# Three moves in the order of a two-layer graph kernel: one gate's sums, one product step's pieces, the late gates' last operations

## The chip, the cores and the metric

The kernel runs on one core of one Trainium2 chip. Its time is the device time of one execution in microseconds (us). Three runs of the kernel before gave 2016.03, 2013.95 and 2015.03 us; the median, 2015.03 us, is the time that the change is compared with. TensorE (PE), VectorE (DVE), ScalarE (ACT), GpSimd (POOL) and SyncE (SP, which only issues DMAs here) each run their own list of instructions in order; what one engine needs from another it waits for by semaphores.

## The reference

64 graphs of 256 nodes with 256 features go through two layers, each with a residual and a layernorm:

```python
x = _layernorm(x + _L0_gnn_ref(x, adj, ...))
# layer 0: deg = adj.sum(-1); norm_adj = deg**-0.5 * adj * deg**-0.5 (rows, columns)
#          ((norm_adj + alpha * I) @ x) @ W.T + b
x = _layernorm(x + _L1_gnn_ref(x, mask, ...))
# layer 1: h = relu(bn1(conv1(xT)));  h = bn2(conv2(h))       17 taps over the nodes
#          x_conv = relu(h + xT).T
#          s = x @ w_se.T + b_se;  A = exp(-|s_n - s_m|**2)
#          msg = relu(x @ w_msg.T + b_msg);  x_nmp = A @ msg
#          GRU: gi = [x_conv, x_nmp] @ w_ih.T,  gh = x @ w_hh.T
#          r, z = sigmoid(gi + gh);  n = tanh(gi_n + r * gh_n)
#          (1 - z) * n + z * x
```

## The kernel before, in words

**Work and groups.** The 64 graphs are taken in four groups of 16 (`Q = 16`), because the 17-tap convolution is computed by a discrete Fourier transform of length 48 over tiles of 32 nodes, with one product for each frequency over the tiles of all 16 graphs of a group. For each graph, `layer0` (L418 on) and `layer1` (L513 on) are generators that are advanced piece by piece; `graphs` interleaves them, so that layer 0 of graph g + 2 runs beside layer 1 of graph g.

- In layer 0, ACT sums the degrees, POOL takes the power deg**-0.5 (`dis`, L438), PE transposes the adjacency matrix (L449), ACT copies it to `adjT` (L450), DVE adds the diagonal (L452), ACT scales x (L467), POOL adds the bias to x_t (L470), PE multiplies (p_hT L475, p_out L485), DVE adds the residual (L491) and `layernorm` follows: two bn_stats (L372), two bn_aggr (L373), `ln_rs` (DVE L374, then a power on POOL, L375), `ln_mr` (L379), and ACT's normalising (L392).
- In layer 1, PE does conv1 (L526), msg (L547) and the transform (p_dft L565); DVE makes the squares (L536 to L539, the last of them `scols`); PE transposes those (p_rows L578), ACT copies them out (L581), PE multiplies distances (p_dist L588), ACT takes exp into `aT` (L589), DVE multiplies aT by the adjacency matrix (L592), and PE sums the messages with it (p_nmp L601). The last DVE and ACT instructions of some of these, of the newest graph, are kept in dictionaries: SQUARED (L539), DIAGONAL (L452), WEIGHED (L592), CONV1, EXP and so on.

**The transform.** For each group q, 12 steps (`PAIRS`) multiply the frequencies (p_k L632). The inverse transform works in place on one tile, VM: `real_transform`, then from step 4 on `complex_begin(step)` (pieces at L686, L687, L691, L692), then `complex_end` (pieces at L718 to L728, L824 and others, and DMAs of its outputs to xc_d at L825). For the first group (q = 0), three pieces of the next group's graphs (`begin`) are run with each step, and the transform's pieces of that step are queued behind the newest graph's SQUARED, DIAGONAL and WEIGHED operations, by `issue_after`. When the steps are over, `paced` advances `complex_end` by a due amount whenever a marked operation of the other work is passed.

**The gate.** `gru(g)` (L966 on) multiplies a graph's inputs by the gate weights as seven half-size products of a Strassen scheme (p_g L982), whose sums of inputs are made ahead on POOL (`sums1` to `sums4`, `input_sums`, L941): gate g makes those of gate g + 1. DVE joins products (L1004, L1014, L1020, L1062), ACT takes two tanh (L1033, L1049), DVE mixes (L1039 to L1048). What remains is the last product and subtraction, `rest()` (L959, L960), and a layernorm of the output (`normed`). Up to the third group, `rest()` and the first part of that layernorm, down to the power on POOL, are run when the next gate begins; in the last group (`g >= B - Q`) they are run in `mixed` and `finished` of the gate itself.

The first gates of a group (`EARLY = (4, 4, 1, Q)`: four, four, one, all) run beside the group's own later graphs or at once; the others of the first three groups, the late gates (4 to 15, 20 to 31, 33 to 47), run beside the steps and graphs of the next group. The order in which each engine gets its instructions is then set by a scheduler from priorities, dependencies and the `issue_after` edges; what stands where in an engine's queue is its result.

Of the kernel before, what the change touches and what calls it, by code (L numbers as in the profile page):

```python
# [26 lines left out]
def kernel(  # L27
# [938 lines left out]
    def gru(g):  # L966

        following = g % Q + 1 < Q  # L970
        inputs, S = GATE.pop(g), SUMS.pop(g)
        G = gate.tile([P, NCH, 2, 4, HD], F32, name="G", bufs=1)
        if following:
            load_gate(g + 1)
        A11, A12, A21, A22 = halves(inputs)

        def product(a, b, p=None):
            first = p is None
            if first:
                p = accbank("p_g")  # L980
            for k in range(HALF):
                nc.tensor.matmul(  # L982
                    p[:, : 3 * HD] if k == 0 else p[:, HD:], a[:, k], wall[:, b, k].rearrange("p t d -> p (t d)"),
                    start=first and k == 0, stop=True, skip_group_check=not first or k > 0,
                )
            return p

        def quarter(c, h):
            return G[:, c, h].rearrange("p t d -> p (t d)")

        p1 = product(A11, B11)
        first = gate.tile([P, 4 * HD], F32, name="first", bufs=1)
        nc.scalar.copy(first, p1)
        p7 = product(S[3], T3)
        yield
        if following:
            sent(g + 1)
        if REST:
            rest()
            next(NORMS[-1])  # L1000
        with tc.issue_after(CONV1[max(CONV1)]) if in_blocks(g) and g < B - Q else ExitStack():
            p6 = product(S[2], T2)
        mark(nc.vector.tensor_add(quarter(0, 1), first, p6), 1)
        nc.vector.tensor_add(quarter(1, 1), quarter(0, 1), p7)  # L1004
        product(A12, B21, p1)
        own = nc.scalar.copy(quarter(0, 0), p1).ins  # L1006
        sooner = following and in_blocks(g + 1) and g < B - Q
        if sooner:
            transposed(g + 1)
        yield  # L1010
        if following and not sooner:
            transposed(g + 1)
        p5 = product(S[1], T1)
        joined = nc.vector.tensor_add(quarter(1, 1), quarter(1, 1), p5)  # L1014
        mark(joined, 1)
        with tc.issue_after(own), tc.issue_after(joined.ins):
            ended()
        load_x1(g)
        product(A22, T4, p7)
        mark(nc.vector.tensor_add(quarter(1, 0), quarter(0, 1), p7), 1)  # L1020
        if following:
            input_sums(g + 1, 3, 1, 2)
        yield
        product(S[4], B22, p5)
        if following:
            input_sums(g + 1, 4)
        if g % Q + 2 < Q:
            load_conv(g + 2)
        x1 = OWN.pop(g)

        def squashed(c, cols=slice(0, 2)):
            rz = G[:, c, cols, GR : GZ + 1, :].rearrange("p h t d -> p h (t d)")
            nc.scalar.activation(rz, rz, AF.Tanh, scale=0.5)  # L1033

        def mixed(part, cols=slice(0, 2)):
            both = G[:, part, cols].rearrange("p c h t d -> p (c h) t d")
            chunks = G[:, part].shape[1]
            r, z, n, i = (both[:, :, j, :] for j in (GR, GZ, GN, GI))
            nc.vector.scalar_tensor_tensor(n, r, 1.0, n, op0=ALU.add, op1=ALU.mult)  # L1039
            i4 = i.rearrange("p (c h) d -> p c h d", c=chunks)  # L1040
            bias = bn_t.rearrange("p (h d) -> p h d", h=2)[:, cols]
            nc.vector.tensor_tensor(
                i4, i4, bias.unsqueeze(1).to_broadcast([P, chunks, bias.shape[1], HD]), op=ALU.add
            )
            MIXED[0] = nc.vector.scalar_tensor_tensor(i, n, 0.5, i, op0=ALU.mult, op1=ALU.add).ins
            y = x1[:, part]
            yq = y.rearrange("p c (h d) -> p c h d", h=2)[:, :, cols].rearrange("p c h d -> p (c h) d")
            mark(nc.vector.scalar_tensor_tensor(yq, z, 3.0, yq, op0=ALU.add, op1=ALU.mult), 1)  # L1048
            nc.scalar.activation(i, i, AF.Tanh)  # L1049
            REST.append((z, i, yq))  # L1050
            if g >= B - Q:
                rest()
            return y

        def finished(part, y):
            NORMS.append(normed(g, part, y))
            if g >= B - Q:
                next(NORMS[-1])

        if g < B - 1:  # L1060
            squashed(1)
            mark(nc.vector.tensor_add(quarter(0, 1), quarter(0, 1), p5), 1)  # L1062
            squashed(0)
            finished(slice(0, NCH), mixed(slice(0, NCH)))
            yield
            return

        top, lower = slice(0, 1), slice(1, 2)
        squashed(0, top)
        y = mixed(top, top)  # L1070
        st = small.tile([P, NCH, nc.vector.BN_STATS_DIM], F32, name="ln_st")
        nc.vector.bn_stats(st[:, 0, :], y[:, 0, :HD])
        squashed(1)
        y1 = mixed(lower)
        nc.vector.tensor_add(quarter(0, 1), quarter(0, 1), p5)
        squashed(0, lower)
        mixed(top, lower)
        with tc.issue_after(MIXED[0]):
            finished(lower, y1)
        nc.vector.bn_stats(st[:, 1, :], y[:, 0, HD:])  # L1080
        with tc.issue_after(RESTED[0]):
            ended()
        run(normed(g, top, y, st))
        yield
# [198 lines left out]
    def gates(q, part):  # L1283

        for i in part:
            if i == 0:
                load_conv(q * Q)
                load_gate(q * Q)
                yield
                load_conv(q * Q + 1)  # L1290
                sent(q * Q)
                yield
                yield
                transposed(q * Q)
                input_sums(q * Q, 3, 1, 2, 4)
                yield
            yield from gru(q * Q + i)

    def nothing():
# [22 lines left out]
    for q in range(NQ):  # L1322
        first = (q + 1) * Q
        more = q + 1 < NQ
        end = complex_end(q)
        if more:
            if q:
                others = [take(late, 3 if i % 3 == 0 else 2) for i in range(AHEAD)]
            else:
                others = [nothing() for _ in range(AHEAD)]  # L1330
                ALONE.update(range(first, first + AHEAD))
            TILES[0] = V2
            begin = graphs(first, range(AHEAD), others)
        KBANK[0] = bank if q else accbank
        sums(0)
        real = real_transform()
        for step in range(STEPS):
            if step < 4:
                run(products(step))
            else:  # L1340
                run(merge(products(step), take(real, 1 if q else 0)))
                if q:
                    run(complex_begin(step))
            if q:
                run(take(late, (0, 1, 1, 1, 1, 1, 2, 1, 2, 1, 2, 1)[step] if more else 0))
            else:
                run(take(begin, 3))
                if step >= 4:
                    with ExitStack() as behind_graphs:
                        for done in (SQUARED, DIAGONAL, WEIGHED):  # L1350
                            behind_graphs.enter_context(tc.issue_after(done[max(done)]))
                        run(take(real, 1))
                        run(complex_begin(step))
        run(real)
        if not q:
            run(paced(begin, end, RATES[q]))
        elif more:
            run(paced(chain(merge(take(late, 20), take(begin, 6), 3), begin), end, RATES[q]))
        else:
            run(paced(late, end, RATES[q]))  # L1360
            run(end)
        if more:
            run(late)
            run(end)
            TILES[0] = V
            early = gates(q, range(EARLY[q]))
            others = [take(early, 6 if q == 0 else 2 if q == 1 or i >= Q - 4 else 0) for i in range(Q)]
            if q == 0:
                others[AHEAD] = with_gates(early)
            run(graphs(first, range(AHEAD, Q), others))  # L1370
            run(early)
            if q == 0:
                scope, AHEAD, V2 = open_ahead(6)
                ctx.enter_context(scope)
            late = gates(q, range(EARLY[q], Q))
        else:
            run(gates(q, range(Q)))
# [55 lines left out]
```

## Time and profile before

| | |
|---|---|
| median of three runs | 2015.03 us |
| profiled execution | 2015.05 us |
| its span, first to last instruction | 2013.3 us |
| around the span | 1.75 us |
| busy: PE, DVE, ACT | 1978.1, 1394.0, 972.3 us |
| busy: POOL | 678.7 us |
| granted TensorE clock, mean | 0.998 |
| p_g products (L982), both forms | 532.9 + 406.4 us |
| p_k products (L632) | 169.8 us |
| aT (L592), 64 times | 696 ns each |
| POOL's power of ln_rs (L375), 129 times | 751 ns each |

The profile is of one execution. Its timeline gives the start and the duration of each instruction from the span's start; a line in it can merge several like instructions. A wait is the time for which an engine had nothing to run, put down to the operation that came last. Names such as x1.21 mean the tile x1 of graph 21.

### The profile page before, as it was taken

How to read it: one execution, taken by the hardware profiler on the slowest of the kernel's cores; microseconds unless marked ns; L12 is line 12 of the kernel's file. 1: busy time of each engine (PE TensorE's matmuls, PEld its weight loads, DVE VectorE, ACT ScalarE, POOL GpSimd, SP SyncE). 2: the span in 40 equal slices, each digit the busy share in tenths (PEclk: the TensorE clock that was granted, in tenths of full speed). 3: DMA queues.
4: the chain of work that ended last, by engine and by line, in shares of the span. 5: the costliest groups of instructions: out<-in, count | busy, mean ns of one | idle time of the engine just before them, and what ended most of it. 6: DMA issues, size and time to landing. Idle time of an engine off the chain costs nothing.

```text
span 2013.3 us, 26520 instructions
## 1 busy us (share of the span) xinstructions
PE 1978.1 (98%) x8191; PEld 1440.6 (72%) x8191; DVE 1394.0 (69%) x3208; ACT 972.3 (48%) x2325; POOL 678.7 (34%) x650
## 2 busy tenths in 40 slices
PE   8999999999999999999999999999999999999998
PEld 7888888878677666777777766778878655555554
DVE  6344448776667888865446789874338999787887
ACT  6666744567442234566653233557752233333333
POOL 4444312222523243323331234332220344344443
PEclk9999999999999999999999999999999999999999
DMA  5667657444447654443335664434229554543331
GB/s 152 201 216 219 217 184 236 162 142 140 132 140 219 197 139 121 130 120 108 104 109 190 215 177 132 121 110 142 100 74 304 151 141 120 136 94 95 97 89 61
DMA packets 256946, 298.88 MB, mean 148 GB/s; under 512 B 70486, under 2 KB 199260, under 8 KB 256806
## 3 DMA queue, kind: packets, MB, share of 16 engines
q1 hardware_dynamic: 195942, 200.45, 34.1%
q10 hardware_dynamic: 44480, 67.32, 9.4%
q0 software_dynamic: 16384, 29.40, 6.6%
q8 instruction: 67, 1.10, 0.2%
q14 instruction: 73, 0.60, 0.1%
HBM read 193.97 MB, written 103.08 MB: 148 GB/s over the span
## 4 chain that ended last, share of the span: by engine, by line
PE 81%; DVE 12%; ACT 2%; DMA 2%; issue 1%; POOL 1%; SPq 0%; ACTq 0%; POOLq 0%; DVEq 0%
PE p_g L982 34%; PE p_k L632 11%; PE p_hT L475 5%; PE p_out L485 5%; PE p_nmp L601 5%; PE p_conv L526 4%; PE p_msg L547 4%; PE p_dft L565 4%; PE p_u L349 2%; PE p_dist L588 2%; PE p_x1T L506 1%; PE p_adjT L449 1%; DVE VM L686 1%; DVE ln_st L372 1%; DVE VM L687 1%
## 5 line engine op out<-in xcount | busy, mean ns | idle before, releaser
L982 PE MATMUL p_g<-wall,sums 128*128 128x384 f32 x1536 | 532.9, 487 | 1.8 <-DVE G L1014 1.8
L982 PEld LDWEIGHTS p_g<-wall,sums 128*128 128x128 f32 x1536 | 285.4, 190 | 187.8 <-issue 8.3
L982 PE MATMUL p_g<-wall,inputs 128*128 128x384 f32 x1152 | 406.4, 488 | 5.4 <-DVE G L1004 5.2
L982 PEld LDWEIGHTS p_g<-wall,inputs 128*128 128x128 f32 x1152 | 215.9, 190 | 159.4 <-DVE G L1004 18.8
L375 POOL TENSOR_TENSOR ln_rs<-ln_rs,neg_half 128x2 f32<-128x2 f32 x129 | 96.7, 751 | 568.7 <-DVE ln_rs L374 436.3
L941 POOL TENSOR_TENSOR sums<-inputs 128x384 f32<-128x384 f32 x128 | 151.2, 1181 | 262.4 <-PE p_g L982 239.1
L592 DVE TENSOR_TENSOR aT<-aT,adjT 128x512 f32<-128x512 f32 x64 | 44.5, 696 | 200.6 <-ACT aT L589 200.4
L632 PE MATMUL p_k<-u,VM 128*128 128x256 f32 x736 | 169.8, 380 | 2.1 <-ACT ab L678 1.5
L470 POOL TENSOR_TENSOR x_t<-x_t,b_t 128x512 f32<-128x512 f32 x64 | 101.8, 1590 | 204.9 <-ACT x L467 106.4
L632 PEld LDWEIGHTS p_k<-u,VM 128*128 128x128 f32 x736 | 138.9, 190 | 24.1 <-ACT ab L678 4.0
L392 ACT ACTIVATE x_g<-x_g,ln_mr,ln_rs 128x256 f32<-128x256 f32 x127 | 69.4, 593 | 158.7 <-DVE ln_mr L379 157.3
L1033 ACT ACTIVATE G<-G 128x512 f32<-128x512 f32 (+1 forms) x129 | 81.0, 628 | 125.6 <-DVE G L1062 87.3
L475 PE MATMUL p_hT<-adjT,x 128*128 128x256 f32 x512 | 122.7, 382 | 3.8 <-ACT x L467 2.2
L526 PE MATMUL p_conv<-wc,xn 128*128 128x259 f32 x512 | 124.5, 384 | 0.7 <-issue 0.7
L485 PE MATMUL p_out<-w,hT 128*128 128x256 f32 x512 | 121.5, 380 | 2.7 <-DVE x L491 1.9
L601 PE MATMUL p_nmp<-aT,msg 128*128 128x256 f32 x512 | 121.3, 380 | 1.9 <-DVE aT L592 1.9
L547 PE MATMUL p_msg<-wmsg,xn 128*128 128x256 f32 x512 | 121.3, 379 | 0.0
L1006 ACT COPY G<-p_g 128x512 f32<-128x512 f32 x64 | 37.4, 585 | 172.4 <-PE p_g L982 111.4
L941 POOL TENSOR_TENSOR sums<-inputs,sums 128x384 f32<-128x384 f32 x64 | 73.2, 1143 | 135.1 <-PE p_g L982 135.0
L565 PE MATMUL p_dft<-fwd,h 128*128 128x240 f32 x512 | 114.3, 366 | 0.0
L526 PEld LDWEIGHTS p_conv<-wc,xn 128*128 128x128 f32 x512 | 97.8, 192 | 20.9 <-issue 0.9
L485 PEld LDWEIGHTS p_out<-w,hT 128*128 128x128 f32 x512 | 95.0, 190 | 21.1 <-ACT hT L480 2.4
(179 smaller groups left out, 3583.7 us busy)
## 6 DMA issues: line engine op xcount, KB each, us to landing
u<-ud SPq DMA_DIRECT2D x284, 256.0 KB
xn_d<-xn ACTq DMA_DIRECT2D x64, 512.0 KB
inputs<-xn_d SPq DMA_DIRECT2D x64, 512.0 KB
ud<-u_set POOLq DMA_DIRECT2D x39, 480.0 KB, 6.2
adj_t<-in_adj_dram SPq DMA_DIRECT2D x64, 256.0 KB
x_t<-in_x_dram SPq DMA_DIRECT2D x64, 256.0 KB
x_d<-x ACTq DMA_DIRECT2D x64, 256.0 KB
xc_d<-VM SPq DMA_DIRECT2D x64, 256.0 KB
```

Source lines behind the costliest of these rows:

```text
L375: nc.gpsimd.tensor_tensor(rs[:, : len(chunks)], rs[:, : len(chunks)], neg_half[:, : len(chunks)], op=ALU.pow)
L470: BIASED[g] = nc.gpsimd.tensor_tensor(x_t, x_t, b0_t.unsqueeze(1).to_broadcast([P, NCH, D]), op=ALU.add).ins
L475: AGGREGATE[g] = nc.tensor.matmul(p[:, k, :], x1[:, mc, k * P : (k + 1) * P], adjT[:, mc, 1 - mc : 3 - mc, :].rearrange("p n q -> p (n q)" ...
L485: out0 = nc.tensor.matmul(p[:, c, :], hT[:, k, c * P : (c + 1) * P], w0[:, k, :], start=k == 0, stop=k == DCH - 1)
L526: CONV1[g] = nc.tensor.matmul(p, x1T[:, k, c * P : (c + 1) * P], wc1[:, k, :], start=k == 0, stop=k == DCH - 1).ins
L547: nc.tensor.matmul(p[:, c, :], x1T[:, k, c * P : (c + 1) * P], wmsg[:, k, :], start=k == 0, stop=k == DCH - 1)
L565: nc.tensor.matmul(p[:, t0 * FL : t1 * FL], h[:, c, k * P : (k + 1) * P], fwd[:, first : first + t1 - t0, :].rearrange("p t f -> p (t f)") ...
L601: nc.tensor.matmul(p[:, k, :], msg[:, mc, k * P : (k + 1) * P], aT[:, mc].rearrange("p n q -> p (n q)"), start=mc == 0, stop=mc == NCH - 1,)
L632: nc.tensor.matmul(p[:, j * D : (j + 1) * D], v[:, k, :], u[:, k, :], start=k == 0 and j == 0 and not onto, stop=k == DCH - 1, skip_group_ ...
L941: nc.gpsimd.tensor_tensor(S[i], x, y, op=op)
L982: nc.tensor.matmul(p[:, : 3 * HD] if k == 0 else p[:, HD:], a[:, k], wall[:, b, k].rearrange("p t d -> p (t d)"), start=first and k == 0, ...
L1033: nc.scalar.activation(rz, rz, AF.Tanh, scale=0.5)
```

## The change

Three edits. In the first, the sums of gate 33's inputs (33 is the second gate of the third group) are no longer made during gate 32 but when gate 33 begins. In the second, in the last step of the first group's products, `begin` is advanced beyond its three pieces until the newest WEIGHED operation is one of a later graph; the transform's pieces of that step are then queued behind that one. In the third, the condition under which `rest()` and the first part of the output's layernorm are run at the gate itself is widened from the last group to all gates that are not early ones (`at_once`).

```diff
@@ gru(g)
         following = g % Q + 1 < Q
+        at_once = g >= B - Q or g % Q >= EARLY[g // Q]
...
-        if following:
+        soon = following and g != 2 * Q
+        if soon:
             input_sums(g + 1, 3, 1, 2)
         yield
         product(S[4], B22, p5)
-        if following:
+        if soon:
             input_sums(g + 1, 4)
...
             REST.append((z, i, yq))
-            if g >= B - Q:
+            if at_once:
                 rest()
             return y
...
             NORMS.append(normed(g, part, y))
-            if g >= B - Q:
+            if at_once:
                 next(NORMS[-1])
@@ gates(q, part)
+            if q * Q + i == 2 * Q + 1:
+                input_sums(q * Q + i, 3, 1, 2, 4)
             yield from gru(q * Q + i)
@@ the loop over the steps
                 run(take(begin, 3))
+                weighed = max(WEIGHED)
                 if step >= 4:
                     with ExitStack() as behind_graphs:
+                        while step + 1 == STEPS and max(WEIGHED) == weighed:
+                            next(begin)
                         for done in (SQUARED, DIAGONAL, WEIGHED):
                             behind_graphs.enter_context(tc.issue_after(done[max(done)]))
                         run(take(real, 1))
```

## The prediction

> **What bounds the kernel now.** The page comes first: it gives busy time by engine and, at its fourth part, the chain of work that ended last.
>
> ```profile
> PE 1978.1 (98%) x8191; PEld 1440.6 (72%) x8191; DVE 1394.0 (69%) x3208; ACT 972.3 (48%) x2325; POOL 678.7 (34%) x650
> ...
> PE 81%; DVE 12%; ACT 2%; DMA 2%; issue 1%; POOL 1%; SPq 0%; ACTq 0%; POOLq 0%; DVEq 0%
> ```
>
> TensorE (PE) is busy 98% of the span and its order of instructions is the same in both programs: laid side by side, all of its instructions stand in the same places. So the change can win or lose only at points where PE waits. I read those next, in the view of the waits, for PE alone:
>
> ```profile
> PE p_g L982 <- DVE G L1004: 5.2, 9, 1.2
> PE p_hT L475 <- ACT x L467: 2.2, 6, 0.5
> PE p_nmp L601 <- DVE aT L592: 1.9, 2, 1.8
> ...
> PE p_rows L578 <- DVE scols L539: 0.8, 1, 0.8
> PE p_dist L588 <- ACT dist_r L581: 0.7, 1, 0.7
> ```
>
> The columns are total us, times and longest. All PE waits together come to about 26 us, some 10 of them in the start-up, and only one is large at the place of the second edit: p_nmp waits 1.8 us for aT. The timeline of that moment says why (DVE, then PE; start, duration):
>
> ```profile
> 369.93 0.61 DVE L452 SCALAR_TENSOR_TENSOR adjT<-ident,adeg,adjT 128x128 f32<-128x128 f32 x2 [0.90 <-ACT adjT L450]
> ...
> 371.91 1.65 DVE L686 TENSOR_TENSOR VM<-VM 128x512 f32<-128x512 f32 x1
> ...
> 377.69 0.68 DVE L592 TENSOR_TENSOR aT<-aT,adjT 128x512 f32<-128x512 f32 x1
> 378.30 0.68 DVE L686 TENSOR_TENSOR VM<-VM 128x512 f32<-128x512 f32 x1
> ```
>
> ```profile
> 378.43 0.48 PE L601 MATMUL p_nmp<-aT,msg 128*128 128x256 f32 x1 [1.78 <-DVE aT L592]
> ```
>
> DVE works off transform pieces (L686 to L692) from 370.46 to 377.69, and only then does aT of graph 19 come, although ACT's exp had its input ready at 374.36 + 0.84 = 375.20. PE's p_nmp waits for it. An operation that lasts 0.68 holds DVE's queue for 0.61 (377.69 to 378.30), and I count with such spacings below.
>
> **Edit 1** (sums of graph 33) moves no instruction on any engine: POOL's sums come in the same order in both programs. 0.
>
> **Edit 2** (last step of the first transform behind graph 19's aT rather than graph 18's). In the new DVE order aT.19 stands directly behind adjT.21's two diagonals, and the pieces behind it. What goes: aT is done by 375.26 + 0.68 = 375.94, ahead of PE, whose p_out ends at 376.3; so p_nmp.19 starts there, and the 1.95 us gap in PE's issue (the wait of 1.78 and a little more) is gone. What comes: DVE has nothing to do from 370.5 to 375.2, 4.7 us. The pieces that filled it are now queued from 375.87 on, ahead of and between x1.21's layernorm. By the new order and the spacings of the rows: two pieces to 377.09; x1 #0 0.40; 686, 691, 687, 692, 686 at 0.61, 0.33, 0.61, 0.33, 0.33 to 379.70; x1 #1 and 687 to 380.43; then 1.14, bn 0.36, 1.14, aggr 0.10, bn 0.36, 0.61, aggr 0.10, deg 0.08, 0.61: ln_rs at 384.93, against 382.62 before. POOL's power takes 0.71 and ln_mr followed 0.98 behind ln_rs, so ln_mr is at 385.9 (383.60 before). ACT then normalises x1.21 (1.0 us for two from 386.1), does msg (0.49) and scales x1.22 (0.50 to its first half): p_hT.22 at 388.1, against 386.38. PE gains 2 us at 376 and loses them and 1.7 more at p_hT. **+1.7.**
>
> In the new POOL order dis.22 stands ahead of ln_rs.21, and it would start at 384.45, inside a DVE piece that runs from 384.32 to 385.0. The row of before for that: POOL's power at 362.71 took 1.08, with DVE's 686 begun at 362.55, where 0.71 is usual; all five powers that began inside such a DVE operation of 0.68 took 1.08 to 1.13, and those that began ahead of one 0.70 to 0.72. So I add 0.4. **+2.1 together** (from -1.95, if the backlog hides, to +2.7).
>
> [...]
>
> Behind it, the closing pieces of the same transform stand differently beside graphs 20 to 27. Before, PE lost 0.42 + 0.70 (graph 21), 0.42 (22), 0.55 + 0.70 (23), 0.18 (25) and 0.40 (26) at p_rows and p_hT, about 3.4 us. A rule that fits these seven: the stall is DVE's piece time behind aT and ahead of ln_mr, less about 1.9 us of slack. Applied to the new order it gives 0.15, 0.75, 0.3, 1.2, 0.2, 0.7, 0: about 3.3. **0, plus or minus 1.** SP's loads and writes swap neighbours here (x_t, adj_t of graphs 24 to 31, needed several graphs later): 0.
>
> **Edit 3** (last operations of the late gates at once). For 28 of the 39 late gates the scheduler had put L959 and L960 there already, and nothing moves. The others, one by one:
>
> - Gates 4, 12, 20, 28: no PE wait within reach (at gate 12 ln_mr is done 2.6 us before its use). 0.
> - Gate 13: L960 (0.61) and one bn stand ahead of scols; p_rows.34 goes from 821.60 to 822.15. **+0.55** (0 to 0.6). Gate 29, its twin, lies under a PE gap of 0.77 that another operation makes: 0 (to +0.5).
> - Gates 15 and 31: the costliest. DVE before, at gate 15:
>
> ```profile
> 891.88 0.74 DVE L372 BATCH_NORM_STATS2 ln_st<-x 128x6 f32<-128x256 f32 x2
> 892.54 0.17 DVE L373 BATCH_NORM_AGGREGATE ln_mv<-ln_st 128x2 f32<-128x6 f32 x1
> 892.62 0.66 DVE L959 SCALAR_TENSOR_TENSOR G<-G 128x512 f32<-128x512 f32 x1
> ...
> 893.92 0.16 DVE L374 TENSOR_SCALAR ln_rs<-ln_mv 128x2 f32<-128x2 f32 x1
> ...
> 894.90 0.16 DVE L379 SCALAR_TENSOR_TENSOR ln_mr<-ln_mv,ln_rs 128x2 f32<-128x2 f32 x1 [0.49 <-POOL ln_rs L375]
> ```
>
> These are x1.39's statistics, with the gate's L959 and L960 between. In the new order L959, L960, the gate's own two bn, two aggr and ln_rs come first: 0.66 for the bn, 0.16 for the aggr and 0.08 more, so x1.39's ln_rs is at 895.0 instead of 893.92, and on POOL two powers (the gate's and dis.40) stand ahead of it, from 894.85: 0.71 + 0.67 + 0.71, ln_mr at 897.0, 2.1 later. ACT has taken adjT.40 ahead of it by then and loses 0.5 less; p_rows.38 goes from 896.71 to 897.8, p_hT.40 from 898.28 to 899.3. **+1.05 each, +2.1** (0 to 4.1, the full delay of ln_mr).
>
> - Beside gate 32 gate 31's statistics no longer stand there. POOL before:
>
> ```profile
> 1480.05 1.00 POOL L941 TENSOR_TENSOR sums<-sums,inputs 128x384 f32<-128x384 f32 x1
> 1481.13 1.00 POOL L941 TENSOR_TENSOR sums<-inputs,sums 128x384 f32<-128x384 f32 x1
> 1482.08 0.71 POOL L375 TENSOR_TENSOR ln_rs<-ln_rs,neg_half 128x2 f32<-128x2 f32 x1
> ```
>
> The new order has x1.63's power ahead of the third sum, 1.0 earlier; the two PE waits of 0.8 and 0.7 above (0.94 and 0.88 as gaps in PE's issue) hang on it one after the other. **-1.0** (-1.1 to 0). At gate 16 POOL's order changes alike, but PE shows no gap there: 0.
>
> - Gates 34, 38, 39, 42: L959, L960 and bn now alternate with pieces, which takes bubbles of about 0.1 between dependent operations out; the waits on L1004 behind them shrink by 0.17 once and 0.1 twice. **-0.35** (-0.35 to 0).
>
> **Sum:** 0 + 2.1 + 0 + 0.55 + 2.1 - 1.0 - 0.35 = +3.4 on the profiled execution's 2015.05 us (span 2013.3 and 1.75 around it), which is the median's 2015.03 too: **2018.4 us.** A measurement of this kernel can tell 0.2%, 4.0 us, from no change, so the bounds of the verdict are 2011.0 and 2019.05; the forecast lies within them.
>
> **Rivals.**
> 1. Slower beyond 0.2%: the backlog of DVE is handed on. The 4.7 us that DVE idles ahead of aT.19 are repaid, by my count, within graph 20. If the graphs 21 to 25, where PE lost 3.4 us already, have less slack than 1.9, each piece left over (0.61 or 1.14) adds its length at a p_hT. Two or three pieces are +2.2, 2020.6 us. It decides from 0.65 us on, one piece. For it speaks that all seven of those waits are DVE's; against it that the transform's pieces end beside the same graph 27 in both orders.
> 2. The wait simply goes. p_nmp.19's 1.95 is won, p_hT.22 is not late because PE's own backlog covers x1.21, and gates 15 and 31 hide behind ACT's new order: -1.95 - 1.0 - 0.35 = -3.3, 2011.75 us; with 1 us from graphs 20 to 26 as well it is 2010.75, beyond 0.2%. Against it: p_hT.22 waited for ACT before already (0.21 in the timeline), so there is no cover.
> 3. It does nothing that counts. Edit 1 and 28 gates move nothing, and the terms of both signs cancel: 2015.0, give or take 1.
>
> **Chances.** Forecast (2016 to 2019.05) 0.43, rival 1 0.33, rival 2 0.12 (half of it below 2011.0), rival 3 0.12. So faster by over 0.2% is 0.06, within 0.2% 0.06 + 0.12 + 0.43 = 0.61, slower 0.33. The range runs from 2013.0, which leaves out about 0.08 of rival 2, to 2021.0, which leaves out about 0.12 of rival 1: the sum of the upper ends there (graph 20 +0.6, gates 15 and 31 +2.0) is 2021.0.
>
> **What would show it.** Right: in the new profile p_nmp's wait on aT is gone from the list, p_hT.22 starts at about 388.5 with a wait of about 4 us on ACT's x, POOL shows dis.22 at 1.1 us, the waits of p_rows on scols show two new ones of about 1 us near gates 15 and 31, and the two gaps beside gate 32 are gone. Wrong: if p_hT.22's wait is under 2 us the backlog hides (rival 2); if p_rows and p_hT of graphs 21 to 25 lose over 4 us in sum it is handed on (rival 1); if neither gate 15 nor 31 shows a wait, ACT's new order covers the powers.

## The result, and the profile after

The changed kernel took 2020.4 us in the median of seven runs (2019.71 to 2021.59), against 2015.03 us; the ratio is 1.0028 with a 95% interval of 1.0018 to 1.0037. That is 5.4 us more: slower, by 0.28% (0.18% to 0.37%). The forecast was 2018.4 us, the range 2013.0 to 2021.0.

The first line of the page, then PE's waits, answer to those shown of before:

```profile
PE 1981.4 (98%) x8191; PEld 1441.9 (71%) x8191; DVE 1387.2 (69%) x3208; ACT 972.8 (48%) x2325; POOL 671.0 (33%) x650
```

```profile
PE p_rows L578 <- DVE scols L539: 5.2, 4, 3.0
PE p_hT L475 <- ACT x L467: 4.4, 7, 1.2
PE p_g L983 <- DVE G L1005: 2.8, 4, 1.2
...
PE p_nmp L601 <- DVE aT L592: 0.4, 2, 0.3
```

The wait of p_nmp on aT is nearly gone, 1.9 to 0.4. In its place p_rows waits 5.2 instead of 0.8, with one wait of 3.0, and p_hT 4.4 instead of 2.2. But the first line holds something that no list of waits shows: PE is busy 3.3 us longer with the same 8191 matmuls. Half of that, 1.6 us, lies at one place, where matmuls were slower (below); the rest is spread in pieces, and the first edit alone, in the order of before, is busy 0.5 us longer as well.

Since PE's order is the same in both programs, the two traces can be subtracted: for each PE instruction, its start after less its start before. Where the difference steps, time was lost or won. (Line numbers behind L968 of the new kernel are higher by the lines added; the kernels of the experiments shift theirs likewise.) The steps, in us, with the runs that did one edit alone beside them:

| stretch, by the time of before | forecast | whole change | first edit alone | second alone | third alone |
|---|---|---|---|---|---|
| 377 to 386.5, up to p_hT.22's start | +2.1 | +2.14 | 0 | +2.13 | 0 |
| 386.5 to 396, the matmuls behind it | 0 | +1.63 | 0 | +1.64 | 0 |
| 396 to 500, graphs 21 to 29 | 0 | +0.21 | 0 | +0.17 | 0 |
| 815 to 830, gate 13 | +0.55 | +1.26 | 0 | 0 | +1.26 |
| 890 to 900 and 1376 to 1385, gates 15 and 31 | +2.1 | +1.20 twice | 0 | 0 | +1.20 twice |
| 1470 to 1490, beside gate 32 | -1.0 | -0.29 | 0 | 0 | -0.29 |
| 1600 to 1780, gates 35, 39, 43 | -0.35 | -0.62 | 0 | 0 | -0.66 |
| everywhere else | 0 | -1.2 | -0.95 | +0.1 | -1.0 |

The last row is not put down to the change: the first edit alone has the same order of instructions on every engine as the kernel before, and its trace still ends 0.95 us off it. Those steps lie mostly at PE's waits for u (a DMA) and at p_g's waits for G in gate 34 and in the last group, and differ from execution to execution. In the last group alone (from 1780 us on), where all of these kernels have the order of before on PE, DVE, ACT and POOL, they sum to anything from -1.8 to +1.4 in the traces of this document.

The moment of the second edit, DVE first, then POOL, then PE:

```profile
375.36 0.69 DVE L592 TENSOR_TENSOR aT<-aT,adjT 128x512 f32<-128x512 f32 x1 [4.68 <-ACT aT L589]
375.97 0.68 DVE L686 TENSOR_TENSOR VM<-VM 128x512 f32<-128x512 f32 x1
...
384.96 0.16 DVE L374 TENSOR_SCALAR ln_rs<-ln_mv 128x2 f32<-128x2 f32 x1
...
386.31 0.16 DVE L379 SCALAR_TENSOR_TENSOR ln_mr<-ln_mv,ln_rs 128x2 f32<-128x2 f32 x1 [0.66 <-POOL ln_rs L375]
```

```profile
384.52 1.09 POOL L438 TENSOR_TENSOR dis<-deg,neg_half 128x2 f32<-128x2 f32 x1 [11.43 <-DVE deg L436]
385.57 0.70 POOL L375 TENSOR_TENSOR ln_rs<-ln_rs,neg_half 128x2 f32<-128x2 f32 x1
```

```profile
382.27 1.78 PE L565 MATMUL p_dft<-fwd,h 128*128 128x240 f32 x8
387.02 0.41 PE L578 MATMUL p_rows<-ident,scols 128*128 128x128 f32 x2 [2.97 <-DVE scols L539]
388.66 3.31 PE L475 MATMUL p_hT<-adjT,x 128*128 128x256 f32 x8 [1.22 <-ACT x L467]
```

DVE idles 4.68 us and then puts aT first; ln_rs is at 384.96 (forecast 384.93), dis takes 1.09 (forecast 1.1), ln_mr is at 386.31 (by the forecast's terms 386.3), p_hT.22 at 388.66 (388.5). Up to here the working held to 0.2 us. But the eight matmuls of p_hT.22 take 3.31 us where they took 1.99 before:

```profile
386.38 1.99 PE L475 MATMUL p_hT<-adjT,x 128*128 128x256 f32 x8 [0.21 <-ACT x L467]
```

The view of stretches, with the granted clock, names the reason. Its columns are the stretch, its length, busy time (and instructions) of PE, PEld, DVE, ACT and POOL, the granted clock, the DMA share and GB/s:

```profile
384.00:387.00 3.00, 0.05 (x1) 0.01 (x1) 2.34 (x13) 0.97 (x2) 1.76 (x2) 1.00 0.00 0
387.00:389.00 2.00, 0.75 (x4) 0.49 (x4) 2.00 (x7) 1.98 (x6) 0.00 (x0) 1.00 0.23 79
389.00:392.00 3.00, 3.00 (x10) 1.94 (x8) 2.05 (x2) 0.63 (x3) 1.39 (x1) 0.53 0.10 35
```

The granted clock is 0.53 from 389 to 392. Matmuls that start 0.216 us apart elsewhere start 0.427 apart here. Before, the same stretch shows 1.00:

```profile
389.00:392.00 3.00, 3.00 (x18) 2.72 (x17) 2.70 (x7) 1.56 (x5) 0.15 (x1) 1.00 0.52 175
```

### The profile page after: what moved, and what is told of

It reads as the page before. It is cut to its first block, busy times and chain, and to the rows that moved or that the text cites. A ratio compares the mean times of both kernels' runs of the same rounds, so it can differ in the third digit from the quotient of the medians.

```text
span 2018.8 us, 26516 instructions
## 1 busy us (share of the span) xinstructions
PE 1981.4 (98%) x8191; PEld 1441.9 (71%) x8191; DVE 1387.2 (69%) x3208; ACT 972.8 (48%) x2325; POOL 671.0 (33%) x650
## 5 line engine op out<-in xcount | busy, mean ns | idle before, releaser
L470 POOL TENSOR_TENSOR x_t<-x_t,b_t 128x512 f32<-128x512 f32 x64 | 97.0, 1516 | 206.2 <-ACT x L467 109.3
```

The costliest lines, as they stand in the source:

```text
L470: BIASED[g] = nc.gpsimd.tensor_tensor(x_t, x_t, b0_t.unsqueeze(1).to_broadcast([P, NCH, D]), op=ALU.add).ins
```

## The experiments

Each is the kernel before with one part of the change, or with a variant of one part; what is added to that is said. Where "..." stands in a piece of code, lines of the same edit are left out. A time is the median of eleven runs, save in experiments 5 and 6. The kernel before ran beside them, with medians of 2015.48 us for experiments 1 to 4, 2014.82 for 5, 6, 11 and 12, and 2015.38 for 7 to 10. The ratio with its 95% interval is not taken from the two medians and can differ a little from theirs.

**1. The first edit alone.**

```diff
+        soon = following and g != 2 * Q
-        if following:
+        if soon:
             input_sums(g + 1, 3, 1, 2)
...
+            if q * Q + i == 2 * Q + 1:
+                input_sums(q * Q + i, 3, 1, 2, 4)
             yield from gru(q * Q + i)
```

> The first edit alone (gate 33's sums made at gate 33). Every engine's list of instructions is in the same order as before, so both theories expect 0 (within 1.0 us of the kernel before), and its trace shows how far two executions of the same order differ step by step. Rival: the place in the program counts although the order does not; then it would be over 2 us from before.

2015.53 us, ratio 0.9997 (0.9988 to 1.0006). No cost can be told; the trace gives the last row of the table above.

**2. The second edit alone.**

```diff
+                        while step + 1 == STEPS and max(WEIGHED) == weighed:
+                            next(begin)
```

> The second edit alone. Theory: most of the loss is here: -1.95 at p_nmp.19, then +3.1 at p_rows.20 and +1.1 at p_hT.22 (waits on VectorE's backlog), +1.6 more because TensorE runs its next matmuls at about half the granted clock after that pause, +0.3 in graphs 20 to 27; together +4.1 us, near 2019.1. Rival: the backlog is handed on through the graphs 21 to 27 (steps there summing to over 2 us) and the slow matmuls are no part of it: +5 or more, or under +2.5 if the slow clock was chance.

2020.07 us, ratio 1.0021 (1.0012 to 1.0030), and +3.94 at graph 29 in its trace, with the slow matmuls again, 0.427 apart:

```profile
388.54 3.61 PE L475 MATMUL p_hT<-adjT,x 128*128 128x256 f32 x8 [1.22 <-ACT x L467]
```

Most of the loss is here. The graphs 21 to 27 add only 0.17, so the backlog was not handed on in this order.

**3. The third edit alone.**

```diff
+        at_once = g >= B - Q or g % Q >= EARLY[g // Q]
...
-            if g >= B - Q:
+            if at_once:
                 rest()
...
```

> The third edit alone. Theory: gate 13 +1.2, gates 15 and 31 +1.1 each, beside gate 32 -0.2, gates 34 to 42 between -1.3 and -0.4: +2 to +3 us together, near 2017.5. Rival: the third edit is what costs the 5.4, by its longer queues at all gates: over +4.

2017.55 us, ratio 1.0010 (1.0001 to 1.0018); the steps are in the table. The rival's +4 is out.

**4. The second edit with PE kept at work in the pause.** Added to the second edit are six matmuls whose result nobody uses; the trace counts each matmul of the program as two (x12).

```diff
         p = bank("p_rows")
+        if g == 20:
+            for _ in range(6):
+                nc.tensor.matmul(p[:, :D], ident, wmsg[:, 0, :], start=True, stop=True)
```

> The second edit alone with six extra 128x128 by 128x256 matmuls on TensorE, whose result is not used, in the wait ahead of p_rows of graph 20 (about 0.42 us each, 2.6 us of the wait of 3.0). Theory, that the pause of TensorE is what lowers its clock: the matmuls of p_hT.22 are back at their usual spacing of 0.21 to 0.22 us and the time is 1.3 to 1.6 us below that of the second edit alone. Rival, that the slow matmuls are chance or come from something else at that moment: no difference (within 0.5 us).

2017.53 us, ratio 1.0012 (1.0003 to 1.0021), 2.5 us below the second edit alone in the median (the runs of the two spread from 2016.03 to 2020.23 and from 2017.87 to 2023.13); by the traces, 1.63 of it at this place. Its stretches, and its p_hT.22:

```profile
384.00:387.00 3.00, 2.71 (x13) 1.91 (x12) 2.34 (x14) 1.06 (x3) 1.76 (x2) 1.00 0.00 0
387.00:389.00 2.00, 0.71 (x4) 0.53 (x4) 2.00 (x6) 1.97 (x6) 0.15 (x1) 1.00 0.38 127
389.00:392.00 3.00, 3.00 (x18) 2.18 (x17) 1.87 (x3) 1.91 (x5) 1.25 (x1) 1.00 0.01 3
```

```profile
386.64 0.44 PE L581 MATMUL p_rows<-ident,scols 128*128 128x128 f32 x2 [0.29 <-DVE scols L539]
388.37 1.99 PE L475 MATMUL p_hT<-adjT,x 128*128 128x256 f32 x8 [1.29 <-ACT x L467]
```

Work whose result nobody uses makes the second edit cheaper: p_rows.20 and p_hT.22 start within 0.1 us of where they do without it, but the clock stays at 1.00 and p_hT.22 is back at 1.99. The slow matmuls are a consequence of PE's pause, not chance.

**5 and 6. Which pause.** Both are variants of experiment 4, each with a single execution, so the traces are what counts. In the first the two extra matmuls stand between p_rows.20 and p_hT.22, in the second three stand ahead of p_rows.20.

```diff
         p = bank("p_hT").rearrange("p (k n) -> p k n", k=DCH)
+        if g == 22:
+            for _ in range(2):
+                nc.tensor.matmul(p[:, 0, :], ident, wmsg[:, 0, :], start=True, stop=True)
```

> The second edit alone with two unused matmuls on TensorE between p_rows.20 and p_hT.22, so only the later, shorter wait (1.2 us) is filled. Theory, that the first pause of 3.0 us lowers the clock by itself: the matmuls of p_hT.22 still stand 0.43 apart and the step after it is still +1.6. Rival, that it needs both pauses together (some 4.5 us of little work): they stand 0.22 apart.

2018.44 us.

```profile
386.94 0.41 PE L581 MATMUL p_rows<-ident,scols 128*128 128x128 f32 x2 [2.98 <-DVE scols L542]
388.57 3.68 PE L478 MATMUL p_hT<-adjT,x 128*128 128x256 f32 x8 [0.36 <-ACT x L467]
```

The matmuls of p_hT.22 are still 0.427 apart and the step is +1.68: the pause of 2.98 us is enough without the second one, of which 0.36 is left.

```diff
-            for _ in range(6):
+            for _ in range(3):
```

> The second edit alone with three unused matmuls (1.3 us) at the start of the pause ahead of p_rows.20, so that 1.6 to 1.7 us of it are left, beside the 1.2 us ahead of p_hT.22. Theory, that only a pause longer than the 2.16 us seen ahead of p_nmp.19 (where the next matmuls stand 0.22 apart) lowers the clock: no slow matmuls, as with six. Rival, that any idle time of this size does it: some stand 0.43 apart.

2018.46 us. My theory fell here. With the pause cut to 1.59 the clock still went down, somewhat later, and stayed down for longer:

```profile
386.28 0.44 PE L581 MATMUL p_rows<-ident,scols 128*128 128x128 f32 x2 [1.59 <-DVE scols L539]
388.01 2.63 PE L475 MATMUL p_hT<-adjT,x 128*128 128x256 f32 x8 [1.29 <-ACT x L467]
```

```profile
389.00:392.00 3.00, 3.00 (x11) 1.59 (x10) 1.43 (x1) 0.77 (x2) 0.88 (x1) 0.54 0.00 0
392.00:396.00 4.00, 4.00 (x12) 3.32 (x12) 2.03 (x5) 1.48 (x4) 0.00 (x0) 0.50 0.17 57
```

From 390 to 396 the matmuls are 0.427 apart and the step is +3.3 instead of +1.6. So the longest single pause does not decide. Two pauses of 1.59 and 1.29 with 0.44 us of work between them lowered the clock; 0.29 and 1.29 with the same between them (experiment 4) did not; nor did a single 1.78 ahead of p_nmp.19 in the kernel before, with full work on both sides (clock 1.00 from 376 to 389). What decides instead, and why the half-filled pause was followed by the longer slow stretch, these runs do not settle.

**7. Only the closing pieces behind graph 19's aT.** The step's own pieces stay where they were, so DVE has work in its pause.

```diff
         if not q:
+            weighed = max(WEIGHED)
+            while max(WEIGHED) == weighed:
+                next(begin)
             run(paced(begin, end, RATES[q]))
```

> Of the second edit only this: the step's own pieces stay behind graph 18's aT, and only the closing pieces of the transform are held until graph 19's aT is issued. VectorE then works through its pause (some 6.2 us of pieces from 370.5), aT.19 comes at 376.6 (before 377.7, with the second edit 375.4), and x1.21's ln_rs at about 382.5, as before. Theory, that the next limit behind p_nmp.19 is p_hT.22, which waits for ln_rs: p_nmp.19 starts 1.0 earlier, p_rows.20 and p_hT.22 give nearly all of it back, no slow clock, 0 to -0.5 together. Rival, that the wait at p_nmp.19 is worth its own size: -1.0.

2013.64 us, ratio 0.9990 (0.9981 to 0.9998).

```profile
378.78 1.99 PE L601 MATMUL p_nmp<-aT,msg 128*128 128x256 f32 x8 [0.72 <-DVE aT L592]
387.27 0.92 PE L475 MATMUL p_hT<-adjT,x 128*128 128x256 f32 x3 [0.74 <-ACT x L467]
```

This execution is 1.42 us late already before the place; relative to that p_nmp.19 starts 1.07 earlier (its wait is 0.72 instead of 1.78). p_hT.22, which waits for x, gives 0.53 of it back (0.74 instead of 0.21; the view ends within it, hence x3), and -0.39 is left at graph 29. The value of the wait at p_nmp.19 is not its size: the next limit behind it takes half. The median is 1.7 us below that of before; what the trace does not place of that stays open.

**8. The closing pieces behind x1.21's layernorm.**

```diff
         if not q:
+            while first + 6 not in MEANS:
+                next(begin)
             run(paced(begin, end, RATES[q]))
```

(MEANS keeps the ln_mr instruction of each graph for this.)

> As the run before, but the closing pieces are held until x1.21's layernorm (ln_mr) is issued, so nothing stands between aT.19 and ln_rs.21 on VectorE. Theory, that both the pause of VectorE and the backlog ahead of ln_rs.21 made the loss of the second edit: p_nmp.19 starts about 1.9 earlier, ln_rs.21 about 3 earlier, p_hT.22 does not wait, and the gain of 1.9 to 2.3 is kept: near 2013 us. Rival, that the backlog is only handed on: the pieces cost it back at graphs 20 to 28, and the time is 2015 or more.

2016.05 us, ratio 0.9997 (0.9988 to 1.0006). Here the rival was right. Neither p_nmp.19 nor p_hT.22 waits any more:

```profile
376.51 1.89 PE L602 MATMUL p_nmp<-aT,msg 128*128 128x256 f32 x8
384.00 1.89 PE L476 MATMUL p_hT<-adjT,x 128*128 128x256 f32 x8
```

p_nmp.19 starts 1.95 earlier and p_hT.22 2.4, the full gain; but from graph 22 on it is given back, in steps of 0.3 to 0.7 at p_hT.23, p_hT.24, p_nmp.24, p_rows.27, p_hT.29 and p_hT.30, until at graph 30 nothing is left (+0.04). DVE's work is the same in amount, and held back it is only repaid later. (The trace then ends 3.29 us behind that of before, with all of it at places where the order is that of before.)

**9. The third edit for gates 33 to 47 alone.**

```diff
+        at_once = g >= 2 * Q + 1
...
```

> The third edit for gates 33 to 47 alone. Theory: the loss at gates 13, 15 and 31 (3.5 us) is gone, the gain at gates 35, 39 and 43 (0.25 each) stays: -0.7 us to the kernel before, near 2014.5, which is hardly to be told from no change. Rival, that the late gates of the third group lose as well: over +1.

2014.88 us, ratio 0.9993 (0.9985 to 1.0002): no change that can be told. Its trace has the three steps of the theory, -0.65 together between 1600 and 1780.

**10. The third edit with gate 32's last sum held behind x1.63's ln_mr.** In the whole change the power of ln_rs does stand ahead of that sum on POOL, as forecast, and the gain is still not there. DVE and POOL after the change:

```profile
1489.73 0.95 DVE L379 SCALAR_TENSOR_TENSOR ln_mr<-ln_mv,ln_rs 128x2 f32<-128x2 f32 x1 [3.28 <-POOL ln_rs L375]
```

```profile
1488.98 0.71 POOL L375 TENSOR_TENSOR ln_rs<-ln_rs,neg_half 128x2 f32<-128x2 f32 x1
1489.67 0.99 POOL L941 TENSOR_TENSOR sums<-inputs,sums 128x384 f32<-128x384 f32 x1
```

ln_mr on DVE, 0.16 in the median, takes 0.95: it started 0.06 behind the sum on POOL and ended with it. The edit, on top of the third, takes the sum out of its place and holds it back:

```diff
...
+        if g == 2 * Q:
+            S[4] = gate.tile([P, HALF, P], F32, name="sums4", bufs=1)
+            with tc.issue_after(MEANS[B]):
+                nc.vector.memset(S[4][0:1, 0, 0:1], 0.0)
+            nc.gpsimd.tensor_tensor(S[4], A12, S[2], op=ALU.subtract)
...
-                input_sums(q * Q, 3, 1, 2, 4)
+                input_sums(q * Q, 3, 1, 2, *(() if q == 2 else (4,)))
```

> The third edit with the last sum of gate 32 held back until ln_mr of x1.63 has been issued (a one-element write by VectorE into its tile, ahead of it, makes POOL wait). Theory, that this sum on POOL blocks ln_mr on VectorE (0.95 us instead of 0.16): ln_mr is back at 0.16, the step at p_rows.62 goes from -0.16 to about -0.9, and the time is 0.8 below the third edit alone. Rival, that ln_mr is long for another reason: it stays at 0.95 and nothing is gained.

2017.03 us, ratio 1.0009 (1.0000 to 1.0018). DVE and POOL here (L540 is scols, L1002 the sum):

```profile
1484.72 0.16 DVE L379 SCALAR_TENSOR_TENSOR ln_mr<-ln_mv,ln_rs 128x2 f32<-128x2 f32 x1 [3.27 <-POOL ln_rs L375]
...
1485.20 1.72 DVE L540 TENSOR_SCALAR scols<-nsq 128x4 f32<-128x4 f32 x1
```

```profile
1485.44 1.43 POOL L1002 TENSOR_TENSOR sums<-inputs,sums 128x384 f32<-128x384 f32 x1
```

The mechanism is as stated: ln_mr is back at 0.16. But the sum then meets scols (1.72 instead of 0.17 to 0.37), on which p_rows.62 waits as well, and PE's step is -0.39 instead of -0.29. The hold-up moved by one instruction, and the expected 0.8 went with it.

**11. The third edit for gates 13, 15 and 31 alone.**

```diff
+        at_once = g >= B - Q or g in (13, 15, 31)
...
```

> The third edit for gates 13, 15 and 31 alone. Theory: the whole loss of the third edit is here: +1.2 at gate 13, +1.1 each at 15 and 31, nothing beside gate 32: +3.3 us, near 2018.7, some 1 us above the third edit as a whole. Rival, that the other 36 gates carry a part of it: +2 or less.

2016.87 us, ratio 1.0011 (1.0002 to 1.0020), 2.0 above the median of before in the same comparison. The steps in the trace are +1.26, +1.20 and +1.20, and -0.29 beside gate 32, which I had not expected to be in this part: it is gate 31's statistics that leave that place. The whole loss of the third edit is in these three gates; at gate 15, in the trace of the whole change, ln_mr waits for POOL's powers and p_rows for scols behind it, as forecast:

```profile
901.86 0.16 DVE L379 SCALAR_TENSOR_TENSOR ln_mr<-ln_mv,ln_rs 128x2 f32<-128x2 f32 x1 [1.61 <-POOL ln_rs L375]
```

```profile
902.44 0.41 PE L578 MATMUL p_rows<-ident,scols 128*128 128x128 f32 x2 [0.82 <-DVE scols L539]
```

The median shows less than the +3.4 of the steps, and the interval (0.4 to 4.0 us) does not tell them apart.

**12. The two parts that did not lose, together** (experiments 7 and 9).

> Two parts that did not lose, together: only the closing pieces behind graph 19's aT, and the third edit for gates 33 to 47. Theory: -0.4 at graphs 19 to 29 and -0.75 at gates 35, 39 and 43: -1.1 us, near 2014.3, at or just below the kernel before. Rival, that parts of this size do not add up: 2015 or more.

2011.41 us against 2014.82 in the same comparison, ratio 0.9985 (0.9976 to 0.9994): faster than both kernels, by more than expected. Its steps are -0.38 at graphs 19 to 29 and -0.65 at gates 35 to 43; the rest lies where the order of instructions is that of before, 1.8 of it at the waits on G in the last group. Steps there vary from execution to execution, but the median of eleven runs is 3.4 us lower as well, so chance in one trace does not account for it. About -1 us of the gain is explained, and the rest is not.

## Why the prediction was right in its range and short in its size

**Right.** Edit 1 at 0, and edit 2 up to p_hT.22: +2.14 against +2.1, with ln_rs, dis, ln_mr and p_hT.22 each within 0.2 us of the time worked out. The 0.4 for POOL's power behind a DVE operation was needed: 1.09 as forecast; the second power there took 0.70. The rows named for the 0.4 were not all, though: beside the five powers of 1.08 to 1.13 two more, at 639.47 and 1123.39 of before, began inside the first of several such DVE operations in a row and took 2.29 each. And the 895.0 given for x1.39's ln_rs does not come out of the terms beside it (894.82); nothing in the sum uses it. Gates 15 and 31 gave +1.20 each against +1.05, and graphs 20 to 27 +0.2 against 0. In the trace p_rows' two waits beside gates 15 and 31 and p_hT.22's later start are there as announced.

**Right in part by luck.** The named places, the rows of the table but the last, add up to +6.7 us: 2021.8 us on the profiled execution of before, above the range's 2021.0; the medians of the three edits alone add up to +6.7 as well. The measured time is inside the range with the -1.2 elsewhere, which was not forecast.

**Wrong in the bound.** The prediction said that the change can win or lose only at points where PE waits. 1.63 us was lost in matmuls that ran slower, with no wait. One of its signs misled too: p_hT.22 waited not about 4 us on ACT's x but 1.22, which it had called the sign of a hidden backlog. The backlog did not hide; 2.97 us of the pause stood one step earlier, at p_rows.20, which waited for DVE's scols and which the working does not name.

**Short by 2 us.** The likeliest case lay below the 0.2% bound and the measured time above it. Three terms failed:

- *"p_hT.22 at 388.1" and what PE does from there.* The forecast put PE's pause at about 4 us itself, and then counted the matmuls behind it at their usual spacing. They were 1.63 slower (clock 0.53). This is the largest miss, and the pause was in my own sum. In the trace of the whole change they stand 0.427 instead of 0.216 us apart, at a clock of 0.50, for some 3.2 us (389.2 to 392.4). A pause of 2.98 did it with one of 0.36 behind it (experiment 5), and two of 1.59 and 1.29 did it (experiment 6).
- *"Gate 13: ... +0.55".* It was +1.26. p_rows.34 was 0.66 late, near the 0.55 worked out from scols; the other 0.61 is p_hT.36, which waits for the second diagonal of adjT.36; two bn now push that behind the start of POOL's x_t:

```profile
826.55 1.02 DVE L452 SCALAR_TENSOR_TENSOR adjT<-ident,adeg,adjT 128x128 f32<-128x128 f32 x1
```

```profile
826.16 1.27 POOL L470 TENSOR_TENSOR x_t<-x_t,b_t 128x512 f32<-128x512 f32 x1 [5.00 <-ACT x L467]
```

  It takes 1.02 instead of 0.34 and ends 0.14 behind the POOL operation. Before, both diagonals were done when POOL began, and a transform piece was held up instead (L720, 1.49), without a wait of PE:

```profile
822.02 0.61 DVE L452 SCALAR_TENSOR_TENSOR adjT<-ident,adeg,adjT 128x128 f32<-128x128 f32 x2
```

```profile
822.64 1.44 POOL L470 TENSOR_TENSOR x_t<-x_t,b_t 128x512 f32<-128x512 f32 x1 [5.00 <-ACT x L467]
```

- *"Beside gate 32 ... -1.0".* It was -0.29 (PE's two waits there are 0.62 and 0.59 instead of 0.77 and 0.72, not gone), because of the same hold-up (experiment 10). I had moved the sum behind the power and not asked what it meets there.

The last two are one omission. The prediction asked which POOL operation a DVE operation holds up (the power of 1.08 at 362.71), and not the reverse (ln_mr 0.95, adjT's diagonal 1.02).

**The rivals.** The time of rival 1 (2020.6) was met, its mechanism was not: graphs 21 to 27 took 0.2, not 2.2. Experiment 8 shows that the mechanism exists, in an order that holds more pieces back. Rival 2 is out by the 2.97 us wait of p_rows.20. Its lowest part, the wait that simply goes, fails in experiment 7 as well: 1.07 won at p_nmp.19 left 0.39.

**What stays open:** what exactly about idle time lowers the clock (experiment 6), why experiments 7 and 12 gain more in the median than their traces place, and the parts of single executions that differ where the order is the same (up to 3.3 us between two traces here).

## What to carry to other kernels

A wait of the bounding engine is worth at most the distance to its next limit (1.07 won left 0.39 in experiment 7): find that one before pricing the edit, and ask where the work that filled the wait will stand afterwards. A pause of TensorE of 2.98 us, and two of 1.59 and 1.29 with 0.44 us of work between, were followed here by matmuls 0.427 instead of 0.216 us apart, for 3 to 6 us: where a change opens such pauses, price the matmuls behind them as well; unused matmuls in the pause were cheaper here than the pause (2017.53 against 2020.07 us). When small operations change places on VectorE or GpSimd, compare their new start times with the other engine's longer operations, in both directions (here dis on POOL 1.09, where 0.70 is its median, begun inside DVE's L687 of 0.69; ln_mr on DVE 0.95 instead of 0.16 beside POOL's sum of 0.99).

## What the runs showed of the hardware

After the change the granted TensorE clock fell from 1.00 to 0.50 behind a pause of 2.97 us and one of 1.22, not at the end of the first: p_rows.20 still took 0.41 us (0.38 before), and the slow matmuls began at about 389.2, some 5 us after the first pause had begun (384.05); from 392.6 the clock was 1.00 again. Two small VectorE operations that started while a GpSimd operation ran took until about that one's end: ln_mr 0.95 instead of 0.16 (it ended 0.02 behind the sum), adjT's diagonal 1.02 instead of 0.34 (0.14 behind x_t). In experiment 10 scols took 1.72 instead of 0.17 to 0.37 and ended with the GpSimd sum, although the profile has it start 0.24 ahead of that (1485.20 against 1485.44).
